# A graph layer on one core: the pool of gathered rows is opened below the memory of the node stage

## The chip, the cores and the metric

The kernel runs on one core of a Trainium2 chip. The metric is the device time of one execution in microseconds (us). The kernel before was timed three times: 4061.18, 4073.2 and 4068.4 us, a median of 4068.4 us. A further execution was recorded by the hardware profiler and took 4061.72 us.

The engines are called as the profile calls them: PE (matrix multiplications; PEld is its weight load), DVE (vector), ACT (scalar), POOL (GpSimd, which here issues the indirect DMAs) and SP (which only issues DMAs). Each engine works through its own queue in order. They meet only where one waits for a semaphore of another or of a DMA. SBUF is the on-chip memory, PSUM the memory that PE writes to.

## The reference

12500 nodes of 160 features (64 scalars and 32 vectors of three components) and 400000 edges, sorted by their destination. Cut to what matters:

```
h  = relu(layernorm(x))
y  = per node: (h @ W_l1) * node_vec1          # the rows that edges gather
s  = per node: (h @ W_sc) * node_vec1
w  = silu(edge_attr_16 @ fc_W1) @ fc_W2        # 192 weights for each edge
mid = products of w, y[src] and edge_attr_4    # per edge: 96 scalars, 96 vectors
z  = sum of mid over the edges with the same dst
out = x + C_S * s + C_X * (z @ W_l2) * node_vec1
```

The step that matters here is y[src]: 400000 rows of 160 floats are fetched from a table of 12500 rows.

## The kernel before

**Node stage** (lines 267 to 410). The 98 tiles of 128 nodes are loaded into `acc`, which stays in SBUF for the whole kernel. For each pair of tiles DVE takes the statistics and centers (`center`, L324 to L326), PE turns and multiplies, ACT scales the result into `ys` (L373), and a DMA from ACT's queue writes a group of eight tiles of y to the table `y_d` in HBM (L376). Behind the 98 tiles come 40 more: `gather_x` fetches, by indirect DMA on POOL (L304, L307), the rows of x and their `node_vec1` for 40 tiles of edges, and the node stage computes y for these directly, in edge order, and writes them to `yr_d` (L378). In the edge stage these 40 tiles are ten blocks, every twelfth from block 12 to block 120 (`made`), which are read with a plain DMA instead of a gather. The temporary memory of this stage is in the pools `nr` (xr, ar and small ones), `ny` (two buffers of `ys`), `ns` and `nd`; below them lies the pool `idx` (dst_i, neg, negb and raw weights).

**Between the stages.** `first_nodes` finds the least destination of each window of three edge tiles on DVE and takes its minimum over the partitions on POOL (L136). `relate` (L138 to L181, in a pool `rel`) then works out on DVE, for all edges, the destination within the window. Its last long steps are L172, L173, L175 and L177.

**Edge stage** (from L436). 3125 tiles of 128 edges are worked in 782 blocks of four. For block b:

- `load(b)` gives the block one of the 12 buffers of the pool `yg` (128 x 4 x 160 floats) and issues four indirect gathers from `y_d` on POOL (L474), one for each tile, or one DMA from `yr_d` on SP (L471) for the ten blocks that were made before. Every eighth block also loads `xe` on SP (L465).
- `weigh(b)` computes the weights w on PE (L505) and scales them on ACT (L421, L422).
- `select(b)` and `products(b)` run on DVE (L536, L538 and L427 to L434). L427, L430, L431 and L432 read yg; L432 is the last of them.
- `sums(b)` sums over the edges on PE (L556), and ACT takes the sums out of PSUM (L561, L563).
- Every third block ends a group of windows, which is turned, multiplied, placed and added to `acc` (L571 to L603).

The order on PE, ACT and DVE is written out by hand in the loop at the end (`manual_schedule`); POOL and SP are not in it, and run their DMAs in the order of the program as soon as the framework's waits allow. `load` runs AHEAD = 10 blocks ahead of the sums. With 12 buffers, the first 12 blocks find a buffer that no earlier block used; block b from 12 on takes the buffer of block b - 12, and can be loaded only when the products of b - 12 have read it.

**Memory.** Pools lie on a stack in SBUF. A pool that is opened after another was closed takes the same addresses, and the framework makes the first access to a new tile wait until all accesses to the tiles that lay there are done, DMAs that read them included. From the sizes of the tiles, counted in bytes for each partition from the end of the constants: `idx` 0 to 23584, `nr` on to about 49984, `ny` on to about 70464, then `ns` and `nd` to some 81000. `rel` takes 23584 to about 45600 after the node stage. The edge stage starts at 0 with `selp`, `prod`, `ld` (36864 to 44032) and `ev`, and has `yg` at 47872 to 78592, then `hid` and `post`.

Of the kernel before, what the change touches and what calls it, by code (L numbers as in the profile page):

```python
# [45 lines left out]
def kernel(  # L46
# [71 lines left out]
    tile_i = const.tile([P, NG], I32, name="tile_i")  # L118
    far_i = const.tile([1, 1], I32, name="far_i")
    full = T // WT  # L120
    before = ctx.enter_context(ExitStack())
    ip = before.enter_context(tc.tile_pool(name="idx", bufs=1))
    dst_i = ip.tile([P, TP], I32, name="dst_i")
# [312 lines left out]
    with (  # L436
# [1 line left out]
        tc.tile_pool(name="prod", bufs=3) as prod,  # L438
        tc.tile_pool(name="ld", bufs=2) as ld,
        tc.tile_pool(name="ev", bufs=2) as evp,  # L440
        tc.tile_pool(name="yg", bufs=12) as ygp,
        tc.tile_pool(name="hid", bufs=4) as hid,
        tc.tile_pool(name="post", bufs=2) as post,
        tc.tile_pool(name="p_w", bufs=2, space=PSUM) as p_w,
# [214 lines left out]
    with (  # L659
# [11 lines left out]
        with tc.For_i(0, n, 1) as _:  # L671
            with tc.For_i(0, ZR, P) as r:
                nc.sync.dma_start(z_d[ds(r, P), :], zero)
            with tc.For_i(0, TP // GT, 1) as g:
# [15 lines left out]
                yg = fp.tile([P, GT, D], F32, name="f_yg")  # L690
# [102 lines left out]
```

## Time and profile before

| | us |
|---|---|
| median of the three runs | 4068.4 |
| the profiled execution | 4061.72 |
| its span in the profile | 4059.8 |
| last write to `y_d` issued | 134.5 |
| last write to `yr_d` issued | 170.65 |
| first gather of L474 | 175.21 |
| first products (L427) | 207.96 |
| last gather of L474 | 4039.11 |

| engine | busy, us | share of the span |
|---|---|---|
| PE | 3235.3 | 80% |
| POOL | 3018.0 | 74% |
| DVE | 2922.8 | 72% |
| ACT | 2692.2 | 66% |

Times in the trace count from the start of the span. The busy time of POOL leaves out the stretch between two DMA issues in which its sequencer prepares the next one; the profile calls that idle time "issue". So POOL can be occupied all the time and still show 74%. A timeline row has the start, the busy time, the engine, the line, the operation with output and input, and in brackets how long the engine had been idle and what, by the trace, ended it. Where a wait is for several semaphores, that name is the one that came last by the trace, and can be a coincidence.

### The profile page before, as it was taken

The numbers are of one execution on the slowest core, as the hardware profiler recorded it, in microseconds if no ns is written. First come the engines' busy times: TensorE is split into PE (matmuls) and PEld (weight loads), VectorE is DVE, ScalarE is ACT, GpSimd is POOL, SyncE is SP. The second block draws the span as 40 slices with busy tenths as digits, with TensorE's granted clock in tenths as the row PEclk, the third lists the DMA queues.
The fourth block names the chain that finished last, engine by engine and source line by source line (L and its number), as shares of the span: only waits on it lengthen the run. The fifth ranks groups of instructions, "written<-read, shape, count | busy, mean of one in ns | idle before, by whom it ended". The sixth has DMA issues, their size and how long they took to land.

```text
span 4059.8 us, 62554 instructions
## 1 busy us (share of the span) xinstructions
PE 3235.3 (80%) x17505; PEld 2347.5 (58%) x17505; DVE 2922.8 (72%) x7558; ACT 2692.2 (66%) x9543; POOL 3018.0 (74%) x3177
## 2 busy tenths in 40 slices
PE   6588888878787787887877887878777788778777
PEld 5466666555555555555555555555555555555555
DVE  7787777776777777777777777767777777777776
ACT  5477777766666666666666666666666666666665
POOL 7477777777777777777777777777777777777776
PEclk9899999999989989999999999999999989999998
DMA  6333333332322233323233332323232323243233
GB/s 192 88 84 83 80 83 80 76 76 74 77 74 74 74 76 74 77 74 76 72 76 75 75 76 74 74 74 77 74 76 74 76 72 76 75 124 75 72 81 78
DMA packets 244949, 326.49 MB, mean 80 GB/s; under 512 B 67290, under 2 KB 194342, under 8 KB 244342
## 3 DMA queue, kind: packets, MB, share of 16 engines
q0 software_dynamic: 151280, 256.22, 25.7%
q1 hardware_dynamic: 74322, 54.52, 4.7%
q10 hardware_dynamic: 18996, 11.72, 0.9%
q8 instruction: 141, 2.31, 0.2%
q14 instruction: 210, 1.72, 0.1%
HBM read 302.92 MB, written 19.28 MB: 79 GB/s over the span
## 4 chain that ended last, share of the span: by engine, by line
DVE 25%; POOL 23%; DMA 21%; issue 21%; PE 5%; ACT 1%; DVEq 1%; ACTq 0%; POOLq 0%
POOL yg L474 23%; DMA yg<-y_d,src_sb 21%; DVE tmp L429 5%; DVE tmp L427 5%; DVE pr L432 3%; DVE pr L431 2%; DVE acc L603 2%; DVE pr L434 2%; DVE sel L538 2%; PE pz L556 2%; DVE pr L430 2%; DVE sel L536 1%; PE pw L505 1%; PE px L483 1%; DVE place L586 1%
## 5 line engine op out<-in xcount | busy, mean ns | idle before, releaser
L474 POOL DMA_INDIRECT yg<-y_d,src_sb x3085 | 2925.3, 948 | 982.5 <-issue 745.8
L556 PE MATMUL pz<-pr,sel 128*128 128x256 f32 x6250 | 1623.9, 407 | 0.3 <-DVE pr L434 0.3
L421 ACT ACTIVATE pw<-pw,ev 128x96 f32<-128x96 f32 x3125 | 985.3, 315 | 858.3 <-PE pw L505 769.6
L556 PEld LDWEIGHTS pz<-pr,sel 128*128 128x128 f32 x6250 | 1237.4, 208 | 157.6 <-issue 0.9
L505 PE MATMUL pw<-w,hT 64*128 64x192 f32 x6250 | 758.5, 363 | 667.1 <-DVE pr L434 657.5
L427 DVE TENSOR_TENSOR tmp<-yg,pw 128x384 f32<-128x384 f32 x782 | 432.8, 553 | 972.3 <-DMA yg<-y_d,src_sb 970.8
L505 PEld LDWEIGHTS pw<-w,hT 64*128 64x128 f32 x6250 | 514.6, 194 | 1060.9 <-DVE pr L434 893.9
L563 ACT ACTIVATE zs<-pz 32x64 f32<-32x64 f32 x3126 | 669.9, 214 | 41.8
L429 DVE TENSOR_REDUCE tmp<-tmp 128x128 f32<-128x384 f32 x782 | 463.7, 593 | 27.0
L538 DVE TENSOR_TENSOR sel<-sel,pw 128x384 f32<-128x384 f32 x782 | 432.7, 553 | 27.0
L561 ACT ACTIVATE zs<-pz 32x192 f32<-32x192 f32 x1042 | 337.8, 324 | 148.3 <-PE pz L556 125.7
L432 DVE TENSOR_TENSOR pr<-pw,yg 128x384 f32<-128x384 f32 x782 | 428.8, 548 | 0.0
L483 PE MATMUL px<-xe,w 32*128 32x512 f32 x782 | 301.0, 656 | 81.8 <-issue 72.7
L488 ACT ACTIVATE hT<-px 128x512 f32<-128x512 f32 x391 | 218.5, 595 | 179.8 <-PE px L483 172.9
L431 DVE TENSOR_TENSOR pr<-pw,yg 128x256 f32<-128x256 f32 x782 | 324.1, 414 | 0.0
L430 DVE TENSOR_TENSOR pr<-pw,yg 128x256 f32<-128x256 f32 x782 | 323.8, 414 | 0.0
L536 DVE TENSOR_TENSOR sel<-iota,pw 128x128 f32<-128x128 f32 x782 | 218.8, 280 | 58.0 <-ACT pw L422 57.6
L580 PE MATMUL px<-wc,za 128*128 128x96 f32 (+1 forms) x1566 | 257.3, 305 | 0.4 <-ACT za L573 0.4
L580 PEld LDWEIGHTS px<-wc,za 128*128 128x128 f32 x1566 | 211.6, 205 | 62.2 <-issue 45.2
L434 DVE TENSOR_TENSOR pr<-pw,tmp 128x128 f32<-128x128 f32 x782 | 220.4, 282 | 0.0
L594 PE MATMUL px<-os,place 128*128 128x160 f32 x1044 | 219.0, 334 | 0.5 <-ACT os L583 0.5
L603 DVE SCALAR_TENSOR_TENSOR acc<-px,a_sb,acc 128x160 f32 x522 | 198.5, 380 | 12.2 <-PE px L594 2.7
(97 smaller groups left out, 1742.0 us busy)
## 6 DMA issues: line engine op xcount, KB each, us to landing
yg<-y_d,src_sb POOLq DMA_INDIRECT x3085
xe<-in_e SPq DMA_DIRECT2D x784, 32.0 KB
y_d<-ys ACTq DMA_DIRECT2D x12, 640.0 KB
acc<-in_x SPq DMA_DIRECT2D x11, 640.0 KB
out<-acc SPq DMA_DIRECT2D x11, 640.0 KB
raw<-in_e SPq DMA_DIRECT2D x32, 192.0 KB
yr_d<-ys ACTq DMA_DIRECT2D x5, 640.0 KB
yg<-yr_d SPq DMA_DIRECT2D x10, 320.0 KB
```

The lines of the kernel that those rows point to most:

```text
L421: nc.scalar.activation(pw[:, k, 0:96], pw[:, k, 0:96], AF.Copy, scale=ev[:, k, 0:1])
L427: nc.vector.tensor_tensor(tmp[:, :n, 0:3, :], y1, wt[:, :n, NW:NW + 3].unsqueeze(3).to_broadcast([P, n, 3, M1]), ALU.mult)
L429: nc.vector.tensor_reduce(tmp[:, :n, 3, :], tmp[:, :n, 0:3, :].rearrange("p t c u -> p t u c"), AX.X, ALU.add)
L430: nc.vector.tensor_mul(pr[:, :n, 192:PC], wt[:, :n, 96:160], yg[:, :n, 0:M0])
L431: nc.vector.tensor_mul(pr[:, :n, 0:M0], wt[:, :n, 0:M0], yg[:, :n, 0:M0])
L432: nc.vector.tensor_mul(pr[:, :n, 96:192].rearrange("p t (c u) -> p t c u", c=3), wt[:, :n, M0:96].unsqueeze(2).to_broadcast([P, n, 3, M1]) ...
L474: nc.gpsimd.indirect_dma_start(out=yg[:, k, :], out_offset=None, in_=y_d, in_offset=bass.IndirectOffsetOnAxis(ap=src_sb[:, t:t + 1], axis=0))
L505: nc.tensor.matmul(pw[:, k, 0:NW], hT[r, o:o + P], w2[r, :], start=True, stop=True)
L538: nc.vector.tensor_tensor(sel[:, :, 0:3, :], sel[:, :, 3:4, :].to_broadcast([P, n, 3, WN]), wt[:, :n, NW:NW + 3].unsqueeze(3).to_broadcast ...
L556: nc.tensor.matmul(pz[:, 0:PC], sels[g][:, t % TG, :, :], pr[:, k, :], start=t % WT == 0, stop=last)
L563: nc.scalar.activation(zs[:, 192 + M0 * c:192 + M0 * (c + 1)], pz[WN * c:WN * (c + 1), 192:PC], AF.Copy)
L580: nc.tensor.matmul(po[:m, lo:hi], za[:, k, :m], wc[:, k, lo:hi], start=k == 0, stop=k == 1)
```

## The change

The pool `yg` is no longer opened with the other pools of the edge stage, but ahead of the pool `idx`, and stays open to the end of the kernel. Its 12 buffers of 2560 bytes for each partition then lie at 0 to 30720 by the count above, directly behind the constants, and `idx`, the node stage, `rel` and the other pools of the edge stage all lie 30720 bytes higher. No other pool ever uses the addresses of `yg`. `hid` and `post` follow `ev` directly. The instructions and their order in the program are the same.

```diff
     full = T // WT
+
+    ygp = ctx.enter_context(tc.tile_pool(name="yg", bufs=12))
     before = ctx.enter_context(ExitStack())
     ip = before.enter_context(tc.tile_pool(name="idx", bufs=1))
...
         tc.tile_pool(name="ev", bufs=2) as evp,
-        tc.tile_pool(name="yg", bufs=12) as ygp,
         tc.tile_pool(name="hid", bufs=4) as hid,
```

## The prediction

> **What bounds the kernel now.** I read the groups of the page first, then busy time by stage, then POOL's own timeline.
>
> ```profile
> L474 POOL DMA_INDIRECT yg<-y_d,src_sb x3085 | 2925.3, 948 | 982.5 <-issue 745.8
> L427 DVE TENSOR_TENSOR tmp<-yg,pw 128x384 f32<-128x384 f32 x782 | 432.8, 553 | 972.3 <-DMA yg<-y_d,src_sb 970.8
> ```
>
> The 3085 gathers take 948 ns each, and the first DVE instruction of a block waits 970.8 us in all for their DMAs. DVE is starved by the gathers. Is POOL itself full? Busy time by stage (columns: window; its length; PE, PEld, DVE, ACT, POOL busy with their counts; granted clock; DMA share; GB/s):
>
> ```profile
> 208.00:276.00 68.00, 64.59 (x368) 46.95 (x369) 62.03 (x159) 56.16 (x203) 51.41 (x55) 0.95 0.34 85
> 276.00:4040.00 3764.00, 3030.20 (x16247) 2186.61 (x16246) 2692.50 (x6857) 2521.16 (x9079) 2847.03 (x3011) 0.94 0.31 77
> ```
>
> From 276 us on there are 3011 gathers in 3764 us: 1.250 us each, which is 0.95 busy and the 0.30 of "issue" that stands ahead of every one. POOL never pauses, so from there the time is a count of gathers. Only in 208 to 276 are PE and DVE busy nearly all the time: there they work off blocks that were gathered in advance, at 3.66 us a block (L427 of block 0 starts at 207.96, of block 17 at 270.18), against 4 x 1.25 = 5.0 us that POOL needs for one. So what counts is when POOL starts, and whether it is stopped afterwards. Its timeline:
>
> ```profile
> 128.86 3.33 POOL L136 PARTITION_ALL_REDUCE negb<-neg  x1 [6.08 <-DVE h L326]
> 175.21 1.47 POOL L474 DMA_INDIRECT yg<-y_d,src_sb  x1 [43.03 <-DVE lim L164]
> 176.99 4.06 POOL L474 DMA_INDIRECT yg<-y_d,src_sb  x1 [0.30 <-issue]
> 181.35 3.14 POOL L474 DMA_INDIRECT yg<-y_d,src_sb  x1 [0.30 <-issue]
> ...
> 188.55 3.01 POOL L474 DMA_INDIRECT yg<-y_d,src_sb  x1 [0.30 <-issue]
> 191.87 0.95 POOL L474 DMA_INDIRECT yg<-y_d,src_sb  x1 [0.31 <-issue]
> ...
> 243.15 0.94 POOL L474 DMA_INDIRECT yg<-y_d,src_sb  x1 [0.30 <-DVE pr L432]
> ```
>
> POOL is idle for 43.03 us ahead of the first gather. The name L164 is a coincidence, I think: that DVE step writes `lim`, which lies below 45600, and yg starts at 47872. The DMA columns name a better candidate:
>
> ```profile
> 135.00:136.00 1.00, 0.55 (x5) 0.38 (x5) 0.93 (x4) 0.79 (x2) 0.00 (x0) 1.00 0.25 69
> 136.00:137.00 1.00, 1.00 (x12) 1.00 (x10) 1.00 (x2) 0.00 (x0) 0.00 (x0) 1.00 0.00 0
> ...
> 172.00:173.00 1.00, 0.00 (x0) 0.00 (x0) 0.92 (x4) 0.00 (x0) 0.00 (x0) 1.00 1.13 363
> 173.00:174.00 1.00, 0.00 (x0) 0.00 (x0) 0.97 (x3) 0.00 (x0) 0.00 (x0) 0.94 0.47 148
> 174.00:175.00 1.00, 0.00 (x0) 0.00 (x0) 0.95 (x3) 0.00 (x0) 0.00 (x0) 0.50 0.00 0
> ```
>
> The last write from ys to yr_d, issued at 170.65, moves data until about 173.5 (half of that window); the gather starts 1.7 us later. ys lies where yg will lie. The data that the gather needs, y_d, is complete much earlier: its last traffic ends just before 136.
>
> **The change, part by part.** Nothing is added or removed; instructions and bytes are the same. Three things move.
>
> 1. *Start of the gathers.* The wait for node-stage memory goes; next in line is the wait for y_d. The last bytes at about 135.9 and the same 1.7 us give 137.6. Bounds: 135.1, when the last issue to y_d ends, and 139.1, the 4.56 us from yr_d's issue to its gather, put behind y_d's last issue at 134.5. POOL is free at 132.2, behind L136; the 6.08 us of idle time before L136 may be a switch of its program, and the same again after it would give 138.3. I take 137.6, the like-for-like row: 37.6 us earlier.
>
> 2. *How much of the head start can be kept.* Buffers limit it. Blocks 0 to 11 are 48 gathers; block 12 comes from yr_d on SP (issued at 210.30 after products of block 0, needed near 252, hidden). Gather 49 is block 13's, and needs the buffer of block 1, free after L432 of block 1. That end is set by another path: xe can be loaded only when L177 is done with the memory of `rel` (both move by 30720 bytes, so that wait stays), then raw, ev, hT, L421, L536:
>
> ```profile
> 187.30 3.44 DVE L177 SCALAR_TENSOR_TENSOR drel<-over,drel 128x3125 f32<-128x3125 f32 x1
> 190.81 7.33 SPq L465 DMA_DIRECT2D xe<-in_e  x16
> 207.96 0.56 DVE L427 TENSOR_TENSOR tmp<-yg,pw 128x384 f32<-128x384 f32 x1
> 212.92 0.55 DVE L432 TENSOR_TENSOR pr<-pw,yg 128x384 f32<-128x384 f32 x1
> ```
>
> So gather 49 can start at 212.92 + 0.55 + 0.30 = 213.8. Before, it started at 243.15 (17 have started by 203.13, then one each 1.25 us). The difference is 29.4 us. POOL must have done its 48 by then: the 80 gathers of the node stage took 111.5 us (11.24 to 122.78, beside DVE), 1.394 each, so 28 are done from 137.6 to 176.8; 6 more to 191.9, as slow as they were there before; the last 14 at 1.25 end at 209.4. The cover is 4.4 us: a start up to that much later costs nothing, and POOL stands still for that time instead. If all the gathers up to 191.9 go at the rate of the first eight (17.9 us, 2.24 each), POOL reaches gather 49 at 221.6 and the gain is 21.5. At 1.25 throughout it is done at 197.6 and nothing is gained by that. I take the first, its row being the same kind of gather beside the same DVE work.
>
> 3. *What the earlier gathers do to DVE.* They now run beside the last node steps and all of `relate`, on whose end gather 49 depends. The rows for L326 alone (20 to 122 with gathers beside, 133 to 166 without):
>
> ```profile
> 20.00:122.00 102.00, 28.23 (x86) 0.97 0.54 154
> 133.00:166.00 33.00, 10.49 (x36) 0.90 0.23 74
> ```
>
> 328 ns against 291 ns: 37 ns x 32 such steps after 137.6 = 1.2 us. DVE is busy 23.15 of 24 us in 167 to 191, so lateness goes through to gather 49. Bounds: 0 (a gain is excluded, no DVE work goes away), and L326 at 1.65 us as it was beside L136: 1.36 x 32 = 43 us. The nearest row is the gathers' own: 1.2 us. In the trace it is the gather that is held instead: 4.06, 3.14 and 3.01 us beside L172, L173 and L177.
>
> The Trainium skill has a rule that speaks against the change ("SBUF — State Buffer", section "Who interferes with whom"): a DVE copy or tensor_scalar in a two-port mode and a POOL instruction lock each other out, and whichever starts second blocks fully. By an estimate from that rule an L326 that meets POOL at random would wait 0.36 us (0.95 of every 1.25 us occupied, half of 0.95 left), 11 us over 32 steps, and the sum would be a gain of 18 instead of 28. The 37 ns of the row speak for the row.
>
> *Later.* POOL must not be stopped again. Block n needs the products of block n - 12. The tightest is block 15: block 3's L432 ended at 222.25, block 14 is issued at 223.8, a cover of 1.5 us. At block 25, after the second made block, it is 259 against 270. The backlog is used up near block 44, about 370 us; until then PE and DVE must hold under 5.0 us a block, and 3.66 is what they did. Were that cover gone, each block would cost its excess over 5.0. The end (20.7 us from the last gather to the end of the span) is as before.
>
> **Sum.** 29.4 - 1.2 = 28.2 us. The profiled execution of 4061.7 becomes 4033.5; the median of the runs is 6.7 higher, 4068.4, and becomes 4040.
>
> **Rivals.**
>
> - *The wait stays* (4068): what held the first gather was not the memory of the node stage but something unmoved. For it: the trace names DVE L164. Against: the DMA columns, and no gather reads what L164 writes. 6 in 100.
> - *POOL comes late* (4047, to 4056 if it also starts 8 us late): DVE starves the gathers as in 177 to 192, so that the 48 aren't done at 213.8. For it: three gathers of over 3 us; against: these stood beside 3.4 us steps, node steps are 0.3 us. 10 in 100.
> - *Slower: POOL holds DVE.* The gathers delay L326 as L136 did, to 1.65 us; `relate` and gather 49 come 43 us later: 29.4 - 43 = -14, so 4082. It decides from 29.4 / 32 = 0.92 us for each step on; the 86 steps beside gathers showed 0.04. 4 in 100, with any other lateness of that size.
> - *The whole head start* (4031): products of block 1 come earlier too, and 37.6 us count. It needs xe before L177 is done. 3 in 100.
>
> **How the numbers follow.** That leaves 77 in 100 for the forecast, 4040, with its own range of 4031 to 4048: runs of one kernel lay 6 us to either side, and the lateness is known to some us. For 8 in 10 with the rivals' nearer ends: 4029 to 4054. A measurement here can tell about 0.3%, 12 us. Faster by more than that: forecast, most of "POOL late" and the whole head start, 0.88. Within it: the wait stays, and a part of "POOL late", 0.07. Slower: 0.05.
>
> **What would show it.** First gather of L474 near 137.6; 48 of them by about 209, and none stretched past the DVE step beside it; then one idle time of some 4 us that ends with L432; the gather of block 13 near 215 instead of 243.15; L427 of block 0 near 209; DVE's first wait for yg after about 370 instead of 275; from then 1.25 us a gather, and the last gather near 4011. Wrong, if the first gather still starts near 175, if L326 goes over 0.6 us, or if a second idle time of POOL appears.

## The result and the profile after

The changed kernel takes 4040.8 us (median of four runs, 4039.3 to 4044.1), beside 4067.8 us for the kernel before: 27.0 us less, a ratio of 0.9934 with a 95% interval of 0.9919 to 0.9950. The forecast was 4040, 28 us less. The profiled execution took 4041.36 us with a span of 4039.5; its span is 20.3 us shorter than that of the profiled one of before, and a section below shows where the difference between 20 and 27 comes from.

Two lines further down than before, since the change adds two lines, the groups of the profile page look almost the same (L475 is the gather, L429 the first step of the products):

```profile
L475 POOL DMA_INDIRECT yg<-y_d,src_sb x3085 | 2929.8, 950 | 958.0 <-issue 749.9
L429 DVE TENSOR_TENSOR tmp<-yg,pw 128x384 f32<-128x384 f32 x782 | 432.2, 553 | 952.2 <-DMA yg<-y_d,src_sb 951.5
```

Still 3085 gathers of 0.95 us and DVE waiting for them: the bound did not change, only when it begins. POOL's timeline shows that:

```profile
128.61 3.33 POOL L138 PARTITION_ALL_REDUCE negb<-neg  x1 [6.77 <-DVE st L326]
138.49 1.19 POOL L475 DMA_INDIRECT yg<-y_d,src_sb  x1 [6.56 <-DMA y_d<-ys]
...
176.53 0.95 POOL L475 DMA_INDIRECT yg<-y_d,src_sb  x1 [0.30 <-issue]
...
180.42 3.03 POOL L475 DMA_INDIRECT yg<-y_d,src_sb  x1 [0.30 <-issue]
183.76 3.13 POOL L475 DMA_INDIRECT yg<-y_d,src_sb  x1 [0.31 <-issue]
...
190.95 3.01 POOL L475 DMA_INDIRECT yg<-y_d,src_sb  x1 [0.30 <-issue]
...
204.28 0.94 POOL L475 DMA_INDIRECT yg<-y_d,src_sb  x1 [0.30 <-issue]
216.88 0.95 POOL L475 DMA_INDIRECT yg<-y_d,src_sb  x1 [11.65 <-DVE pr L436]
```

The two bounds of the new start-up stand in the brackets. The idle time of 43.03 us has become one of 6.56, and its end is now the write to y_d that the gather really needs. Then 48 gathers run without a pause, and a second idle time of 11.65 us follows, which before did not exist: block 13 wants the buffer of block 1. The path that frees this buffer is on DVE and SP (L183 ends `relate`, L466 loads xe, L434 of block 1 is the last reader):

```profile
193.08 0.13 DVE L183 TENSOR_SCALAR far_i<-cnt 1x1 int32<-1x1 f32 x1
193.21 8.32 SPq L466 DMA_DIRECT2D xe<-in_e  x16
...
211.12 0.55 DVE L429 TENSOR_TENSOR tmp<-yg,pw 128x384 f32<-128x384 f32 x1
216.06 0.55 DVE L434 TENSOR_TENSOR pr<-pw,yg 128x384 f32<-128x384 f32 x1
```

L434 ends at 216.61 and gather 49 starts 0.27 us later, at 216.88. (The trace names L436, the step behind L434, which does not read yg.) Of the 36.7 us by which the first gather is earlier, gather 49 keeps 243.15 - 216.88 = 26.3.

### The profile page after: what moved, and what is told of

It reads as the page before. It is cut to its first block, busy times and chain, and to the rows that moved or that the text cites. A ratio compares the mean times of both kernels' runs of the same rounds, so it can differ in the third digit from the quotient of the medians.

```text
span 4039.5 us, 62548 instructions
## 1 busy us (share of the span) xinstructions
PE 3237.9 (80%) x17505; PEld 2352.5 (58%) x17505; DVE 2921.0 (72%) x7558; ACT 2690.3 (67%) x9543; POOL 3021.9 (75%) x3177
## 4 chain that ended last, share of the span: by engine, by line
DVE 23%; POOL 22%; issue 20%; DMA 20%; PE 7%; ACT 2%; DVEq 1%; ACTq 0%; POOLq 0%
POOL yg L475 22%; DMA yg<-y_d,src_sb 20%; DVE tmp L431 5%; DVE tmp L429 4%; PE pz L557 3%; DVE pr L434 3%; DVE pr L433 2%; DVE acc L604 2%; DVE sel L539 2%; DVE pr L436 2%; PE pw L506 2%; DVE pr L432 1%; DVE sel L537 1%; PE px L484 1%; ACT pw L423 1%
## 5 line engine op out<-in xcount | busy, mean ns | idle before, releaser
L475 POOL DMA_INDIRECT yg<-y_d,src_sb x3085 | 2929.8, 950 | 958.0 <-issue 749.9
L429 DVE TENSOR_TENSOR tmp<-yg,pw 128x384 f32<-128x384 f32 x782 | 432.2, 553 | 952.2 <-DMA yg<-y_d,src_sb 951.5
L434 DVE TENSOR_TENSOR pr<-pw,yg 128x384 f32<-128x384 f32 x782 | 427.0, 546 | 0.0
L436 DVE TENSOR_TENSOR pr<-pw,tmp 128x128 f32<-128x128 f32 x782 | 217.9, 279 | 0.0
```

Of the source, the lines that this page charges most:

```text
L429: nc.vector.tensor_tensor(tmp[:, :n, 0:3, :], y1, wt[:, :n, NW:NW + 3].unsqueeze(3).to_broadcast([P, n, 3, M1]), ALU.mult)
L434: nc.vector.tensor_mul(pr[:, :n, 96:192].rearrange("p t (c u) -> p t c u", c=3), wt[:, :n, M0:96].unsqueeze(2).to_broadcast([P, n, 3, M1]) ...
L475: nc.gpsimd.indirect_dma_start(out=yg[:, k, :], out_offset=None, in_=y_d, in_offset=bass.IndirectOffsetOnAxis(ap=src_sb[:, t:t + 1], axis=0))
```

## The experiments

The theory had two parts. First, the start: the first gather had waited for the old content of its memory, in the end for the last write out of `ys`. Second, what is kept: the gain is the time by which gather 49 comes earlier, which the number of buffers and the end of the first products set, since after it POOL never stops. The rivals were that something unmoved held the first gather, and that the later part of the gain was lost elsewhere. The first four kernels are set beside 4062.6 us for the kernel before (median of 18 runs), the next four beside 4063.0 (median of 9, on another chip).

### Only ys moved away

```diff
# the kernel before
+    ny = ctx.enter_context(tc.tile_pool(name="ny", bufs=2))
     before = ctx.enter_context(ExitStack())
...
-        tc.tile_pool(name="ny", bufs=2) as ny,
...
-        tc.tile_pool(name="yg", bufs=12) as ygp,
+        tc.tile_pool(name="yg", bufs=11) as ygp,
```

> The kernel before, with only the pool ny (the two ys buffers) opened below idx and 11 instead of 12 yg buffers, to make room; yg stays where it was relative to nr, ns and nd, but no longer lies on ys. Theory (the first gather waited for the last write from ys to yr_d to land): the wait now ends with the last readers of nr, ns and nd, that is the last L373 on ACT or the last center on DVE, so the first gather starts at 167 to 171 us instead of 175.2, and the time is 4 to 8 us shorter. Rival (DVE L164 or something else that was not moved held it): the first gather starts at 175 again, the time is that of before.

Measured: 4058.4 us, beside 4062.6. That is a single run, which can't carry a difference of 4.2 us; the trace is the evidence here. The timeline of ACT, its DMA queue, POOL and DVE (L165 is the step that was L164):

```profile
170.87 0.84 ACT L373 ACTIVATE ys<-po,ra 128x160 f32<-128x160 f32 x2 [0.21 <-PE po L362]
171.74 0.37 ACTq L378 DMA_DIRECT2D yr_d<-ys  x1
172.00 1.89 POOL L474 DMA_INDIRECT yg<-y_d,src_sb  x1 [40.67 <-ACT ys L373]
...
175.41 0.70 DVE L165 TENSOR_SCALAR lim<-off 128x1044 f32<-128x1044 f32 x1
```

The first gather starts at 172.00, 0.29 us after the last L373 and before the write to yr_d can have moved anything: that write was issued only 0.26 us earlier, and the one of before took 2.9 us from its issue to the end of its traffic. In the profile of before the last L373 ended at 170.62 and the gather came 4.59 us later. So the landing of that write was the last 4.3 us of the old wait; some 32 us before it, back to the 138 us at which the changed kernel starts, stood behind the other pools of the node stage. The step that the trace of before had named, L164, starts here only after the gather: it was a coincidence. (172.00 is 1 us later than I had expected, because the last L373 itself ends 1.1 us later in this execution.)

### yg at the front of the edge stage's own pools

```diff
# the kernel before
     with (
+        tc.tile_pool(name="yg", bufs=12) as ygp,
         tc.tile_pool(name="selp", bufs=3) as selp,
...
-        tc.tile_pool(name="yg", bufs=12) as ygp,
```

> The kernel before, with yg only moved to the front of the edge stage's own pools, so that it lies on idx, nr and rel instead of nr, ny, ns and nd; ld then lies on ny instead of on rel. Theory, if the waits go buffer by buffer: buffers 0 to 5 lie on dst_i and neg, which are free by 132, so 24 gathers run from about 138 to 168; buffers 6 to 11 wait for the readers of negb and lim in relate, about 186; gather 49 comes near 218 and the time is 23 to 25 us below before. Rival, if a wait holds until all of the pools below are free: the first gather starts after relate, near 191, gather 49 near 251, and the time is 8 us above before.

Measured: 4072.7 us beside 4062.6, a ratio of 1.0025 (1.0015 to 1.0034): 10 us slower. My guess that waits go buffer by buffer was wrong, and the rival right. The timeline of DVE's last step of `relate` and POOL's first gather:

```profile
192.04 0.13 DVE L181 TENSOR_SCALAR far_i<-cnt 1x1 int32<-1x1 f32 x1
192.98 1.19 POOL L474 DMA_INDIRECT yg<-y_d,src_sb  x1 [59.86 <-DVE far_i L181]
```

yg lies on 0 to 30720 here, and the first block's buffer, wherever it is in that range, is read for the last time before 187 (negb and lim, by L172 and L173, which end at 185.3 in this execution). The gather waited until `relate` had ended, 6.8 us after the last step that reads memory under yg, and `over`, which the last long step reads, does not lie under yg at all. So the wait does not go by single buffers or tiles; it fits a wait for the pools below as a whole. (Which instruction released it isn't shown: the gather starts 0.8 us behind the one that the trace names, and not the 0.3 us seen elsewhere.) This fits the kernel before as well, where even block 0 waited for the last of the `ys` buffers.

### Eight buffers

```diff
# the changed kernel
-    ygp = ctx.enter_context(tc.tile_pool(name="yg", bufs=12))
+    ygp = ctx.enter_context(tc.tile_pool(name="yg", bufs=8))
```

> The changed kernel with 8 yg buffers instead of 12. Theory (what is kept of the head start is set by the number of buffers and by the products of the first blocks): POOL does 32 gathers by about 179 and then stands still until L434 of block 0, at 213; gather 33, which came at 223.13 before, comes at 213.4, so 9 to 10 us of gain are left, 4058. Also, no gather runs beside the second half of relate: if they were what made it late, relate ends nearer to 191 than to 193. Rival (the head start alone counts, buffers don't): 4041 as with 12.

Measured: 4051.3 us beside 4062.6, ratio 0.9972 (0.9962 to 0.9982), 11.3 us less. POOL's timeline, gathers 32 and 33:

```profile
178.76 3.02 POOL L475 DMA_INDIRECT yg<-y_d,src_sb  x1 [0.30 <-issue]
210.99 0.94 POOL L475 DMA_INDIRECT yg<-y_d,src_sb  x1 [29.20 <-DVE pr L436]
```

The first gather is as early as with 12 buffers (138.29), but POOL stands still for 29.2 us after 32 gathers. Gather 33 comes at 210.99 instead of 223.13, 12.1 us earlier, and about that much is measured. (It is 2.4 us before the 213.4 I had expected, because I had taken the end of block 0's products from the profile of after; in this execution L434 of block 0 ended at 210.72.) That the head start alone counts is excluded. On the lateness of `relate` this run can't decide: it ended at 191.51, but the next section but one shows 190.6 with all 48 gathers.

### Thirteen buffers

```diff
# the changed kernel
-    ygp = ctx.enter_context(tc.tile_pool(name="yg", bufs=12))
+    ygp = ctx.enter_context(tc.tile_pool(name="yg", bufs=13))
```

> The changed kernel with 13 yg buffers, all that the node stage leaves room for. Theory: block 13 takes the buffer of block 0 of the second turn, free after L434 of block 0 (213.4) instead of after block 1 (216.6): gather 49 at 213.7 instead of 216.88, 3.2 us less, 4037.6 (below what three rounds can tell, so the trace decides). Rival (another thing stops POOL at 205): it starts again at 216.9.

Gather 49 in POOL's timeline of this kernel:

```profile
211.90 0.94 POOL L475 DMA_INDIRECT yg<-y_d,src_sb  x1 [6.93 <-DVE pr L436]
```

Gather 49 starts 0.27 us after L434 of block 0 (211.08 + 0.55), one block earlier than with 12, as the theory said. Measured: 4030.1 us beside 4062.6, ratio 0.9919 (0.9903 to 0.9936), 32.5 us less. With 12 buffers it was 27.0 and 29.8 us less in two other sets of runs, so the 3.2 us that I expected of the thirteenth buffer can't be told from the times. The trace shows them: L434 of block 1, for which 12 buffers would have waited, ends at 214.83, 3.2 us after that of block 0.

### The changed kernel again, 16 buffers, xe early, and both

These four ran side by side on one chip. The first is the changed kernel without an edit.

> The changed kernel once more, beside the next three on the same chip. Theory: 27 us below before again; the profile again has POOL standing still for about 11 us from 205. If the distance between two gathers differs from execution to execution (1.2503 us in the profile of before, 1.2523 us in that of after), this profile shows another value between 1.250 and 1.254, and 3000 gathers times that difference, some 6 us, is the spread between runs; if 1.2523 belongs to the change, it is 1.252 again in every profile with yg below.

Sixteen buffers, the last four from the memory of the edge stage:

```diff
# the changed kernel
         tc.tile_pool(name="ev", bufs=2) as evp,
+        tc.tile_pool(name="yg2", bufs=4) as ygp2,
...
-            yg = ygp.tile([P, GT, D], F32, name="yg")
+            yg = (ygp if b % 16 < 12 else ygp2).tile([P, GT, D], F32, name="yg")
```

> The changed kernel with four more yg buffers, taken from a second pool in the edge stage's memory (blocks 12 to 15 of every 16 use it), whose old content is free at 175, long before POOL gets there. Theory: POOL finds a buffer for block 13 at 205.2 and for block 16 at 220 (block 0 is free at 213.4), never stands still, and the 11.65 us of idle time go: 11.3 us below the changed kernel, near 4029.5. Rival (the loss is not the buffers but the late products, which DVE and PE cannot make up): 4041.

The memory of xe and raw taken off that of `rel`:

```diff
# the changed kernel
+        tc.tile_pool(name="hid", bufs=4) as hid,
+        tc.tile_pool(name="post", bufs=2) as post,
         tc.tile_pool(name="ld", bufs=2) as ld,
         tc.tile_pool(name="ev", bufs=2) as evp,
-        tc.tile_pool(name="hid", bufs=4) as hid,
-        tc.tile_pool(name="post", bufs=2) as post,
```

> The changed kernel, 12 buffers, with the pools of the edge stage in another order: hid and post ahead of ld and ev, so that xe and raw lie on ny (free near 174) and not on the memory of rel (free at 193). Theory: xe and raw are there before relate ends, products of block 0 start near 200 instead of 211.1, L434 of block 1 ends near 205.5, just when POOL has done its 48; the idle time shrinks from 11.65 us to under 2, and the time to near 4030. Rival (loading xe early collides with the gathers or the path is set by something else in the chain, such as drel or the table load of ACT): products of block 0 stay near 209 to 211, 4039 to 4041.

Both edits together:

> The changed kernel with both: 16 buffers and xe loaded early. Theory: both take away the same idle time of POOL, so together they give no more than either, 4029 to 4030, and POOL runs without a stop from 138 to the end. Rival (they are two separate losses): their gains add up, 4018 to 4020.

Measured, each beside 4063.0 for the kernel before: 4033.2 for the changed kernel (ratio 0.9928, 0.9914 to 0.9941), 4025.4 with 16 buffers (0.9907, 0.9891 to 0.9922), 4026.1 with xe early (0.9908, 0.9892 to 0.9923), 4024.5 with both (0.9905, 0.9890 to 0.9921). Gather 49, the one that follows the first 48, in POOL's timelines of the four.

The changed kernel:

```profile
214.22 0.95 POOL L475 DMA_INDIRECT yg<-y_d,src_sb  x1 [9.11 <-DVE pr L436]
```

With 16 buffers:

```profile
206.91 0.95 POOL L476 DMA_INDIRECT yg<-y_d,src_sb  x1 [0.31 <-issue]
```

With xe early:

```profile
207.98 0.94 POOL L475 DMA_INDIRECT yg<-y_d,src_sb  x1 [1.47 <-DVE pr L436]
```

With both:

```profile
207.82 0.95 POOL L476 DMA_INDIRECT yg<-y_d,src_sb  x1 [0.30 <-ACT zs L565]
```

The idle time of 9.11 us goes with more buffers, or with earlier products (L429 of block 0 starts at 202.21 with xe early, 208.45 without), and the two together give no more than either, as the theory said: 7.8, 7.1 and 8.7 us, where I had expected 11.3 from the longer pause in the profile of after. It was one loss, not two. Sixteen buffers, or the other order of pools, was faster than both kernels here. With the other order all four runs (4023.5 to 4026.3) lie below the five of the changed kernel (4032.1 to 4034.1); with 16 buffers three of four do. The order of pools costs no memory.

### All of them on one scale

How much earlier gather 49 is than the 243.15 of before, beside what the medians show:

| kernel | first gather | products of block 0 | gather 49 | earlier by | median less by |
|---|---|---|---|---|---|
| changed | 138.49 | 211.12 | 216.88 | 26.3 | 27.0 |
| changed, again | 137.36 | 208.45 | 214.22 | 28.9 | 29.8 |
| ys moved away | 172.00 | 208.95 | 240.62 | 2.5 | 4.2 |
| yg at the front | 192.98 | 199.85 | 253.22 | -10.1 | -10.1 |
| 8 buffers | 138.29 | 208.42 | 231.25 | 11.9 | 11.3 |
| 13 buffers | 137.22 | 209.33 | 211.90 | 31.2 | 32.5 |
| 16 buffers | 138.78 | 209.03 | 206.91 | 36.2 | 37.6 |
| xe early | 139.85 | 202.21 | 207.98 | 35.2 | 36.9 |
| both | 140.10 | 199.48 | 207.82 | 35.3 | 38.5 |

Neither the first gather nor the first products predict the time; the start of gather 49 does, within 3.2 us in all nine. Each start is that of one profiled execution, and between the two of the changed kernel it moved by 2.7 us, so a closer match can't be asked for. (Before the products of the first blocks are done, different kernels are ahead by different amounts; by gather 49 POOL has had its last stop in each.)

## Why the prediction was right

**The bound.** Right. From 276 us on POOL had no pause in the kernel before, and has none in the changed one.

**Start of the gathers.** Forecast 137.6 from the end of the traffic to y_d and the 1.7 us that the old gather had stood behind its own DMA; measured 138.49 and, in the second execution, 137.36. The trace now names that write. After the all-reduce POOL was idle until 138.49, so a switch of its program, if there is one, was covered.

**What is kept.** Right in kind: buffers and the products of block 1 set it. The cover was mis-sized. I had given the gathers beside the node stage 1.394 us each and had them done at 209.4, 4.4 us before they would be wanted; the first thirty took (176.53 - 138.49) / 30 = 1.27 each, and all 48 were done at 205.2. The row I took them from contains the additions of s to acc (1.48 us each), and gathers beside them took about 2 us; only a short last addition (0.47 us at 139.65) was left when these gathers ran. POOL stood still for 11.65 us instead of 4.4, which cost nothing, as the step said, but was also the place where more could be had.

**Lateness of DVE.** I had taken 1.2 us for 32 centering steps at 37 ns more. The steps themselves were as forecast (busy time by window of L328 alone, the center's last step, in the changed kernel; the second column with its count is DVE):

```profile
138.00:166.00 28.00, 9.52 (x29) 0.82 0.49 132
```

9.52 / 29 = 328 ns, against 291 before. The whole lateness of the first products was 3.2 us in this execution (211.12 against 207.96). 0.54 of it were there before the first gather ran (the addition of s at 135.50 starts at 136.04), 1.5 more by the start of `relate`, 0.3 in `relate`, and 0.8 behind it, where the 16 issues of xe took 8.32 us instead of 7.33. In the second execution of the same kernel it was 0.5 us. So this term of the sum is smaller than what one execution differs from the next, and its exact size stays open: the `relate` of the three kernels with no gathers before 170 started at 166.80, 167.88 and 168.19, and of the two executions of the changed one at 168.87 and 166.48. In the five variants of it that start lies at 167.40 to 171.42.

The Trainium skill's rule that POOL and DVE lock each other out ("SBUF — State Buffer", section "Who interferes with whom") would have made this term 11 us by the prediction's estimate; the 328 ns do not show it. Nor do longer steps of the same kind: the two TENSOR_SCALAR steps that make `lim` took 0.70 us each beside gathers (L166 and L167 here), as they did in the run with yg at the front, where no gather ran yet. In this trace it is the gathers that are held: three of them took 3.03, 3.13 and 3.01 us beside the long steps L174, L175 and L179, each of which has two inputs in SBUF, and those that ran beside the reduction L177 between them took 0.94 and 0.95.

```profile
179.22 3.40 DVE L174 TENSOR_TENSOR drel<-drel,negb 128x3123 f32<-128x3123 f32 x1
182.66 3.41 DVE L175 TENSOR_TENSOR over<-drel,lim 128x3123 f32<-128x3123 f32 x1
...
186.37 3.41 DVE L177 TENSOR_REDUCE far<-over 128x1 f32<-128x3125 f32 x1
189.69 3.44 DVE L179 SCALAR_TENSOR_TENSOR drel<-over,drel 128x3125 f32<-128x3125 f32 x1
```

So in this trace the two engines also meet where neither waits for a semaphore of the other, which the description of the engines ahead of the prediction leaves out.

**Later.** No second stop appeared. DVE first waits for a gather again at 379.75, where I had put about 370 with the backlog used up; from 276 to 376 PE and DVE work it off with hardly a gap (busy time by window, the columns as in the prediction):

```profile
276.00:376.00 100.00, 99.00 (x587) 72.46 (x585) 95.52 (x247) 89.81 (x327) 75.67 (x80) 1.00 0.34 86
```

**The sum.** 28.2 us against a measured 27.0 and, in the second set of runs, 29.8. The mechanism is right, but a match to 1 or 2 us is partly luck: the profiled execution, which I had put at 4033.5, took 4041.4, and two executions of one kernel differ by more than the term for DVE. The rival of the wait that stays is excluded by POOL's first gather at 138.49, the late POOL by its pause, the held DVE by the 328 ns. "The whole head start" is what 16 buffers or an early xe give: 36 us at gather 49. I had tied that case to earlier products of block 1 alone; more buffers do it too.

**Profile and median.** The spans of the two profiled executions differ by 20.3 us and not 27. Gather 49 is 26.3 us earlier, the last one 20.35 (4018.76 against 4039.11), so 5.9 us are lost over 3036 gathers, spread evenly: 1.2523 us from one to the next instead of 1.2503. This does not belong to the change. The second execution of the changed kernel has 1.2502 from the hundredth gather on, and one of 16 buffers 1.2530, while three other runs of that kernel were 8 to 10 us shorter than the profiled one.

## What to carry to other kernels

A buffer that is fetched ahead should not share memory with the stage before, if the fetching engine is the bound: the wait for that memory (37 of the 43 us here) hides behind a name that the trace infers. The DMA columns and the addresses say what it may be, and moving one pool at a time shows it. The gain of an earlier start is not the head start but what is left of it at the last place where the engine stops afterwards: count the buffers, and the time at which the first one is free again. When a new pause shows up there, more buffers and an earlier consumer are two ways to the same time, and the order in which pools are opened can be the cheaper one.

## What had not been expected of the hardware

The mean distance between two gathers on POOL belongs to one execution and not to the kernel: means from 1.2501 to 1.2530 us over some 3000 gathers in the ten profiles, most of them at 1.2501 to 1.2503. With POOL as the bound, 0.002 us for each gather is 6 us of the time, five times the 1.2 us that the prediction worked out for DVE. What sets it was not looked for. The two sets of runs of the changed kernel differ as well, 4040.8 and 4033.2 us, where before took 4067.8 and 4063.0 beside them.
